# A transformer block in fp32: the last sequence's attention and shared experts moved in front of the routed experts

## The chip, the cores and the metric

The kernel runs on one core of a Trainium2 chip. The metric is the device time of one execution in microseconds. A core has TensorE (PE, matrix products; PEld is its weight load), VectorE (DVE), ScalarE (ACT), GpSimd (POOL) and SyncE (SP). The engines run their own instruction queues in order and wait for each other through semaphores. SP and ACT issue plain DMAs, POOL issues the indirect ones (gathers and scatters of rows).

## The reference

There are 16 sequences of 512 tokens with 256 channels, all fp32. The block normalizes, and adds to its input linear attention with 16 heads, a shared SwiGLU expert and routed experts (two groups of four, two experts of one group for each token):

```python
xn = layernorm(x)                                        # 16 x 512 x 256
q, k = elu(xn @ Wq + bq) + 1, elu(xn @ Wk + bk) + 1
v = xn @ Wv + bv
kv = einsum('bkhd,bkhm->bhdm', k, v)                     # by head, 16 x 16
att = einsum('bqhd,bhdm->bqhm', q, kv) / max(sum(q * sum_k k), 1e-6)
att = att @ Wo + bo
shared = swiglu(xn @ w_in.T) @ w_out.T                   # hidden 512
h = swiglu(xn @ w1.T)                                    # one hidden row for all routed experts
routed = sum over e of (h * w_se[:, e]) @ w2[e].T        # two weights per token are not zero
out = x + att + shared + routed
```

## The kernel before

**Sequences.** A loop over the 16 sequences (`for b in range(B)`, L992) computes for each one: the routed hidden rows `h` (`hidden_rows`, products `phr` on L587), written to the DRAM table `h_d`; the shared expert's hidden values `hs_all` (`hidden`, products `phs` on L613); and the attention. A row of `h_d` has 770 floats: 512 of `h`, 256 of the residual, and two routing weights. Both hidden layers go through `seven`, which forms two-by-two blocks with seven products for each half; its 14 products come in an order written out by hand, and after product number `n` it calls `then(n)`.

The attention needs only a small matrix for each sequence: `summarize` gives `xk` (L681), and `mix` makes of it `pvk` (L694, PE), `vk` (L703 and L708, DVE), `pm` (L713, PE) and `kvo` (L717, ACT). `outputs` then forms the sum of the shared expert and of the attention for a tile of 128 tokens in one PSUM group (L750): four products with `wout_sb` and two with `kvo`, each of which runs as two passes in fp32. `gather` adds that to the residual in `res` (L761) and stores it to `h_d` (L762).

**Routing.** `order` sorts the tokens by the pair of experts that they use, in pieces set between other work by `next(steps_of_order)`. There are 67 tiles of 128 slots that are always needed (`SURE`); a few more are run under `tc.If` if the counts ask for them (`rest`, L1061; its branch shows as L1063).

**Routed tiles.** A `Tiles` object holds two tiles. `rows()` gathers their rows from `h_d` by an indirect DMA on POOL for each tile (L902), into one of four buffers (the reused `qq_all`, `x_all`, `kk_all`, `xn_all`). `turn()` transposes the hidden half to `hT`: twelve copies on ACT (L923), four and three transposes on DVE (L929, L935); there are two `hT` buffers. `sums()` runs eight passes for each tile on PE with the weights of both experts (`py`, L952; `w2_sb` is shown as `w_sb`), then two DVE operations that bring in the gathered residual and weights (L959, L962), then scatters `y` to the output by an indirect DMA on POOL (L965). Rows are gathered three pairs ahead (`AHEAD = 3`), and turned two pairs ahead.

**The last sequence.** After its `hidden_rows`, the last four experts' weights are loaded over the space that held the weights of that layer (`load_expert`, L198, 16 DMAs on SP). Rows of the first three pairs are gathered before `hidden`. Its residual without attention and shared expert has been put into `h_d` early (L999). `mix` follows after four pairs of routed tiles (L1059), and the last sequence's outputs come at the very end: they are added to what the scatters left in the output, which is read back for that (`far`, L1081, `last`, L1088, stored on L1089).

**Order.** Each engine's order is made by a list scheduler of the language from the source order and the dependencies; `keep_in_program_order` fixes the order of the instructions given to it, `issue_after` puts one behind another, and `high_priority` draws instructions forward. PSUM has six banks for `ps_mm` and two for `ps_y`.

Of the kernel before, what the change touches and what calls it, by code (L numbers as in the profile page):

```python
# [10 lines left out]
FP = mybir.dt.float32  # L11
AF = mybir.ActivationFunctionType
ALU = mybir.AluOpType
AX = mybir.AxisListType

P = 128
# [5 lines left out]
def block_kernel(  # L22
# [29 lines left out]
    nc = tc.nc  # L52
    B, S, D = x.shape
# [3 lines left out]
    HID = w_out.shape[0]  # L57
    DH = 16
    KD = D // P
# [449 lines left out]
    def between(b, n):  # L509

        if b + 2 >= B:
            for _ in range(n or 0):
                next(steps_of_order)
# [84 lines left out]

        seven(f"phr_{b}", product, lambda a: a, room, done, lambda n: between(b, then(n)))

    def hidden(b, xs7):

        h = hs_all
        made = []

        def split(a):
            return a.rearrange("p (f j) -> p f j", f=2)

        def product(to, u, i, start, stop):


            for f in range(2):
                tc.keep_in_program_order(nc.tensor.matmul(  # L613
                    split(to)[:, f, :], lhsT=win_in[W7[i]][:, ts(2 * u + f, P)], rhs=xs7[i],
                    start=start and f == 0, stop=stop, skip_group_check=True,
                ))
# [30 lines left out]
    def first_hidden(xnT):  # L647

        more = weight_sums(win_in, win_12)
        for f in range(KH):  # L650
            both = []
            for w in ((win_in[0], win_in[1]), (win_12, win_in[2])):
                ph = ps_mm.tile([P, S], FP, tag="mm", name=f"phs_0_{f}_{len(both)}")
                for k in range(KD):
                    nc.tensor.matmul(
                        ph, lhsT=w[k][:, ts(f, P)], rhs=xnT[:, k, :], start=(k == 0), stop=(k == KD - 1)
                    )
                both.append(ph)
# [27 lines left out]
        nc.scalar.copy(xk, pxk)  # L686
        return xk

    def mix(b, xk, ksb):

        pvk = ps_mm.tile([P, KD, P], FP, tag="mm", name=f"pvk_{b}")
        for c in range(KD):
            for k in range(KD):
                nc.tensor.matmul(  # L694
                    pvk[:, c, :], lhsT=wv_sb[:, k, ts(c, P)],
                    rhs=by_quadrant(xk[:, k, :])[:, c],
                    start=(k == 0), stop=(k == KD - 1),
                )
        vk = one.tile([P, KD, P], FP, tag="vk", name=f"vk_{b}")

        with tc.high_priority():
            for c in range(KD):
                nc.vector.scalar_tensor_tensor(  # L703
                    vk[:, c, :].rearrange("p (q i) -> p q i", i=Q), by_quadrant(ksb)[:, c],
                    bv_sb[:, c : c + 1], pvk[:, c, :].rearrange("p (q i) -> p q i", i=Q),
                    ALU.mult, ALU.add,
                )
            nc.vector.tensor_tensor(  # L708
                vk, vk, headmask.unsqueeze(1).to_broadcast([P, KD, P]), ALU.mult
            )  # L710
        pm = ps_mm.tile([P, KD, D], FP, tag="mm", name=f"pm_{b}")
        for c in range(KD):
            nc.tensor.matmul(  # L713
                pm[:, c, :], lhsT=vk[:, c, :], rhs=wo_sb[:, c, :], start=True, stop=True
            )
# [23 lines left out]

    def outputs(b, t, qT, kvo, hs):  # L740


        if b + 2 < B or (b + 1 == B and t == 0):
            po = ps_y.tile([P, D], FP, tag="py", name=f"po_{b}_{t}")
        else:
            po = ps_mm.tile([P, D], FP, tag="mm", name=f"po_{b}_{t}")
        parts = [(hs[:, f, ts(t, P)], wout_sb[:, f, :]) for f in range(KH)]
        parts += [(qT[:, c, ts(t, P)], kvo[:, c, :]) for c in range(KD)]
        for i, (a, w) in enumerate(parts):
            step = nc.tensor.matmul(po, lhsT=a, rhs=w, start=(i == 0), stop=(i == len(parts) - 1))  # L750
            if b + 1 == B:
                tc.keep_in_program_order(step)
        return po

    def gather(b, res, qT, kvo, hs, placed, then):

        for t in range(NT):
            po = outputs(b, t, qT, kvo, hs)

            with tc.issue_after(placed.ins) if placed and t > 1 else nullcontext():  # L760
                nc.vector.tensor_tensor(res[:, t, 0:D], po, res[:, t, 0:D], ALU.add)  # L761
            nc.sync.dma_start(out=h_d[ts(b * NT + t, P), HID:ROW], in_=res[:, t, :])  # L762
            between(b, then(t))

    def order():

# [225 lines left out]
    for b in range(B):  # L992
        xn, xnT, _ = normed.pop(b)
        res, qq, kk = fronts.pop(b)
        if b + 1 < B:
            fronts[b + 1] = front(b + 1, normed[b + 1][1])
        if b + 2 == B:

            nc.sync.dma_start(  # L999
                out=h_d[ts(b + 1, S), HID:ROW].rearrange("(t p) h -> p t h", p=P), in_=fronts[b + 1][0]  # L1000
            )
            steps_of_order = order()
        if b + 1 == B:
            sums7 = token_sums(b, xnT)
            hidden_rows(b, sums7, {2: 2, 6: 2, 9: 2, 13: 2}.get)

            for e in waiting:
                load_expert(e)
            *lists, filled = next(steps_of_order)
            tiles = [Tiles(list(range(i, min(i + 2, SURE))), *lists) for i in range(0, SURE, 2)]  # L1010
        xk = summarize(b, xn, kk)
        if b == 0:
            sums = key_sum(0, kk)
            queries[0] = attend(0, qq, sums)
        if b + 2 < B:
            normed[b + 2] = normalize(b + 2)
        if b + 3 < B:
            xs[b + 3] = load_x(b + 3)
        if b == 0:
            first_rows(xnT)  # L1020
        elif b + 1 < B:
            sums7 = token_sums(b, xnT)
            hidden_rows(b, sums7, {9: 1}.get)
        ksb, (qT, turned) = sums, queries.pop(b)
        turned()
        if b + 1 < B:
            sums = key_sum(b + 1, fronts[b + 1][2])
# [18 lines left out]
        skip_runtime_bounds_check_because="whole tiles for all tokens, a part of a tile more for a pair",  # L1046
    )

    for i, w in enumerate(tiles[: AHEAD - 1]):

        w.turn(made[i])
    for g, w in enumerate(tiles):
        if g + AHEAD < len(tiles):
            tiles[g + AHEAD].rows()
        if g + AHEAD - 1 < len(tiles):
            tiles[g + AHEAD - 1].turn()
        w.sums()
        if g == AHEAD:
            kvo = mix(B - 1, xk, ksb)  # L1059

    def rest(i):  # L1061
        if i < TILES:
# [8 lines left out]
                    w.sums()  # L1071
                rest(i + STEP)


    first_po = outputs(B - 1, 0, qT, kvo, hs)
    rest(SURE)


    for half, queue in enumerate((nc.sync, nc.scalar)):
        far = work.tile([P, 2, D], FP, tag="hr", name=f"far_{half}", bufs=4)  # L1080
        queue.dma_start(  # L1081
            out=far, in_=out[B - 1, ts(half, 2 * P), :].rearrange("(t p) d -> p t d", p=P)
        )
        for j in range(2):
            t = 2 * half + j
            po = outputs(B - 1, t, qT, kvo, hs) if t else first_po
            y = work.tile([P, D], FP, tag="y", name=f"last_{t}", bufs=4)
            nc.vector.tensor_tensor(y, po, far[:, j], ALU.add)  # L1088
            (nc.sync, nc.scalar)[t % 2].dma_start(out=out[B - 1, ts(t, P), :], in_=y)  # L1089


# [30 lines left out]
```

## Time and profile before

| | |
|---|---|
| median of 3 runs | 1045.91 us (1045.9 to 1046.4) |
| the profiled execution's own time | 1045.97 us |
| its span, first to last instruction | 1044.2 us |
| mean granted TensorE clock | 0.992 |
| PE, DVE, ACT, POOL busy | 1011.8, 787.8, 479.1, 242.3 us |
| sequences, to the last `phs` product | 0 to 784.1 us |
| routed tiles | 792.5 to 1029.4 us |
| the last sequence's outputs and the end | 1029.4 to 1044.2 us |

The lines of a timeline read: start in us, duration, engine, source line, operation, output and inputs by name, shape, and how many instructions were merged; in brackets the idle time of the engine before it and what ended it. In a wait list the numbers are the total in us, how often, and the longest.

### The profile page before, as it was taken

To read this page: it belongs to the slowest core of one execution; us is meant where nothing else is said; L and a number is where in the kernel's file an instruction comes from. 1 tells how busy PE (TensorE), PEld (TensorE's weight loads), DVE (VectorE), ACT (ScalarE), POOL (GpSimd) and SP (SyncE) were. 2 spreads that over 40 slices of the span, in tenths; PEclk is the share of its full clock that TensorE was granted. 3 is DMA by queue.
4 is the path that set the end of the run, shared out by engine and by line. 5 is a ranking of instruction groups with operands and counts; after the bars stand their busy time and mean duration, and the time that the engine had idled before them with its cause. 6 is when DMAs were issued, how large, how long until landed. Compare 5 with 4: busy or idle time off the path is not lost. (4 is left out here: it accounts for less than half of the span.)

```text
span 1044.2 us, 12410 instructions
## 1 busy us (share of the span) xinstructions
PE 1011.8 (97%) x3704; PEld 685.2 (66%) x3704; DVE 787.8 (75%) x1976; ACT 479.1 (46%) x886; POOL 242.3 (23%) x353
## 2 busy tenths in 40 slices
PE   6999999999999999999999999999896999999998
PEld 4566868677786868686777768686672444444445
DVE  5969797978788797878786877868975666666662
ACT  2415353534344352535344443425138666667770
POOL 5202020110202021110202020211022555565541
PEclk9999999999999999999999999999998999999999
DMA  7142624425151523314141313221253445544441
GB/s 217 42 138 87 174 87 116 127 71 151 51 161 49 162 78 87 121 42 141 41 121 56 115 57 114 84 61 61 60 141 127 142 137 154 160 149 149 149 125 69
DMA packets 130436, 114.24 MB, mean 109 GB/s; under 512 B 72605, under 2 KB 114589, under 8 KB 130368
## 3 DMA queue, kind: packets, MB, share of 16 engines
q1 hardware_dynamic: 120080, 77.42, 25.3%
q0 software_dynamic: 8912, 35.21, 11.2%
q10 hardware_dynamic: 1376, 0.80, 0.3%
q8 instruction: 31, 0.51, 0.2%
q14 instruction: 37, 0.30, 0.1%
HBM read 63.52 MB, written 50.27 MB: 109 GB/s over the span
## 5 line engine op out<-in xcount | busy, mean ns | idle before, releaser
L952 PE MATMUL py<-w_sb,hT 128*128 x536 | 233.1, 598 | 8.4 <-DMA w_sb<-in_w 8.4
L952 PEld LDWEIGHTS py<-w_sb,hT 128*128 128x128 f32 x536 | 102.7, 192 | 137.7 <-issue 137.7
L750 PE MATMUL po<-wout_sb,hs_all 128*128 128x256 f32 x512 | 124.9, 382 | 1.9 <-DVE hs_all L572 1.4
L382 POOL TENSOR_TENSOR res<-x_all,bo_sb 128x256 f32<-128x256 f32 x64 | 49.0, 796 | 271.7 <-DMA h_d<-res 204.9
L750 PEld LDWEIGHTS po<-wout_sb,hs_all 128*128 128x128 f32 x512 | 95.8, 191 | 17.4 <-DVE hs_all L572 3.4
L965 POOL DMA_INDIRECT out<-y,goal x67 | 67.8, 1012 | 104.3 <-DVE y L962 95.1
L761 DVE TENSOR_TENSOR res<-po,res 128x256 f32<-128x256 f32 x60 | 25.5, 424 | 74.7 <-PE po L750 72.0
L668 POOL TENSOR_TENSOR k<-kk_all 128x512 f32<-128x512 f32 x16 | 20.9, 1309 | 261.8 <-DVE sm L450 251.9
L750 PE MATMUL po<-kvo,qT 128*128 128x256 f32 x256 | 65.9, 383 | 0.0
L587 PE MATMUL phr_w<-w_sb,ss 128*128 128x512 f32 x120 | 62.2, 600 | 3.6 <-DVE hr L566 2.2
L613 PE MATMUL phs_w<-ss,win_sb 128*128 128x256 f32 x240 | 61.6, 379 | 0.0
L613 PE MATMUL phs_t<-xnT,win_sb 128*128 128x256 f32 x240 | 61.6, 379 | 0.0
L587 PE MATMUL phr_t<-w_sb,xnT 128*128 128x512 f32 x120 | 61.3, 593 | 0.0
L404 PE MATMUL pk<-wkr_sb,xnT 128*128 128x266 f32 x240 | 58.9, 395 | 0.3 <-ACT xnT L305 0.3
L613 PE MATMUL phs_t<-ss,win_sb 128*128 128x256 f32 x240 | 59.1, 379 | 0.0
L587 PE MATMUL phr_t<-w_sb,ss 128*128 128x512 f32 x120 | 59.0, 593 | 0.0
L390 ACT ACTIVATE km<-km 128x1024 f32<-128x1024 f32 x16 | 16.9, 1058 | 90.7 <-DVE km L389 90.7
L681 PE MATMUL pxk<-kk_all,xn_all 128*128 128x256 f32 x256 | 57.9, 379 | 0.0
L923 ACT COPY hb<-qq_all 32x256 f32<-32x256 f32 x108 | 43.4, 402 | 26.2 <-DMA qq_all<-h_d,source 22.8
L415 PE MATMUL pq<-w_sb,xnT 128*128 128x256 f32 x240 | 54.2, 379 | 0.0
L750 PEld LDWEIGHTS po<-kvo,qT 128*128 128x128 f32 x256 | 47.5, 190 | 8.9 <-ACT kvo L717 3.0
L681 PEld LDWEIGHTS pxk<-kk_all,xn_all 128*128 128x128 f32 x256 | 48.6, 190 | 6.6
(215 smaller groups left out, 1936.3 us busy)
## 6 DMA issues: line engine op xcount, KB each, us to landing
h_d<-hr SPq DMA_DIRECT2D x64, 256.0 KB, 2.4
q_d<-qq_all SPq DMA_DIRECT2D x16, 512.0 KB, 2.8
qb<-q_d SPq DMA_DIRECT2D x64, 128.0 KB, 3.0
w_sb<-in_w SPq DMA_DIRECT2D x64, 128.0 KB, 3.5
h_d<-res SPq DMA_DIRECT2D x60, 129.0 KB, 1.9
x_all<-in_x SPq DMA_DIRECT2D x15, 512.0 KB, 5.3
xn_d<-xn_all SPq DMA_DIRECT2D x14, 512.0 KB, 3.5
xb<-xn_d SPq DMA_DIRECT2D x56, 128.0 KB, 3.0
```

Source lines behind the costliest of these rows:

```text
L382: nc.gpsimd.tensor_tensor(res[:, t, 0:D], xt[:, t, :], bo_sb, ALU.add)
L404: nc.tensor.matmul(pk, lhsT=xnT[:, k, ts(t, P)], rhs=wkr_sb[:, k, :], start=(k == 0), stop=(k == KD - 1),)
L415: nc.tensor.matmul(pq[:, t, :], lhsT=xnT[:, k, ts(t2 + t, P)], rhs=wq_sb[:, k, :], start=(k == 0), stop=(k == KD - 1),)
L587: tc.keep_in_program_order(nc.tensor.matmul(to, lhsT=xs7[i][:, ts(u, P)], rhs=w1_in[W7[i]], start=start, stop=stop, skip_group_check=True,))
L613: tc.keep_in_program_order(nc.tensor.matmul(split(to)[:, f, :], lhsT=win_in[W7[i]][:, ts(2 * u + f, P)], rhs=xs7[i], start=start and f == ...
L668: nc.gpsimd.tensor_tensor(k2, kk[:, 0:2, :], kk[:, 2:4, :], ALU.add)
L681: nc.tensor.matmul(pxk[:, c, :], lhsT=xn[:, t, ts(c, P)], rhs=kk[:, t, :], start=(t == 0), stop=(t == NT - 1),)
L750: step = nc.tensor.matmul(po, lhsT=a, rhs=w, start=(i == 0), stop=(i == len(parts) - 1))
L761: nc.vector.tensor_tensor(res[:, t, 0:D], po, res[:, t, 0:D], ALU.add)
L923: nc.scalar.copy(there[ts(q, Q), a - near, 0:n, :], self.hg[ts(a, Q), 0:n, ts(q, W)])
L952: nc.tensor.matmul(py.rearrange("p j d -> p (j d)"), lhsT=self.hT[:, f, ts(j, P)], rhs=w2_sb[:, f, bass.ds(regs[i % TR], 2 * D)], start=(f ...
L965: stored = nc.gpsimd.indirect_dma_start(out=out_rows, out_offset=bass.IndirectOffsetOnAxis(ap=self.goal[:, i : i + 1], axis=0), in_=y, in_ ...
```

## The change

The last sequence is treated like the others: its outputs are added to `res` and stored to `h_d` in front of the routed tiles, and the routed sums bring them to the output with the residual. `mix` is split into `values` and `mix`, which for the last sequence run after products 2 and 8 of `hidden`, with PSUM tiles from `ps_y`. A new `gather_last` does the outputs of all four tiles, first the products with `kvo`, then those with `wout_sb`, in two PSUM banks, with two adds and two stores. Since the rows of the first three pairs are gathered before these stores, they are gathered again afterwards, for their residual part: pairs 0 and 1 in front of the loop over the tiles, pair 2 in its first round, behind the gather of pair 3 and the turn of pair 2. The gather of pair 3 itself keeps its place in the source, which is now behind the stores. The part at the end that reads the output back is gone.

```diff
-    def hidden(b, xs7):
+    def hidden(b, xs7, then=lambda n: None):
...
-        seven(f"phs_{b}", product, split, room, done, lambda n: None)
+        seven(f"phs_{b}", product, split, room, done, then)
         return h, made
...
-    def mix(b, xk, ksb):
-        pvk = ps_mm.tile([P, KD, P], FP, tag="mm", name=f"pvk_{b}")
+    def small_sums(b, shape, name):
+        if b + 1 == B:
+            return ps_y.tile(shape, FP, tag="py", name=f"{name}_{b}"), tc.keep_in_program_order
+        return ps_mm.tile(shape, FP, tag="mm", name=f"{name}_{b}"), lambda step: step
+
+    def values(b, xk, ksb):
+        pvk, pin = small_sums(b, [P, KD, P], "pvk")
...
+        return vk
+
+    def mix(b, vk):
+        pm, pin = small_sums(b, [P, KD, D], "pm")
...
-        nc.scalar.copy(kvo, pm)
+        with tc.high_priority() if b + 1 == B else nullcontext():
+            nc.scalar.copy(kvo, pm)
         return kvo
...
+    def gather_last(b, res, qT, kvo, hs):
+        pos = [ps_y.tile([P, 2, D], FP, tag="py", name=f"po_{b}_{i}") for i in range(NT // 2)]
+        def add(parts, t, begin, end):
+            for i, (a, w) in enumerate(parts):
+                tc.keep_in_program_order(nc.tensor.matmul(
+                    pos[t // 2][:, t % 2, :], lhsT=a, rhs=w, start=begin and i == 0 and t % 2 == 0,
+                    stop=end and i == len(parts) - 1, skip_group_check=True,
+                ))
+        for t in range(NT):
+            add([(qT[:, c, ts(t, P)], kvo[:, c, :]) for c in range(KD)], t, True, False)
+        for t in range(NT):
+            add([(hs[:, f, ts(t, P)], wout_sb[:, f, :]) for f in range(KH)], t, False, True)
+        for i, po in enumerate(pos):
+            to = res[:, 2 * i : 2 * i + 2, 0:D]
+            with tc.high_priority():
+                nc.vector.tensor_tensor(to, po, to, ALU.add)
+            nc.sync.dma_start(
+                out=h_d[ts(b * NT // 2 + i, 2 * P), HID:ROW].rearrange("(t p) h -> p t h", p=P),
+                in_=res[:, 2 * i : 2 * i + 2, :],
+            )
...
-        hs, made = hidden(b, sums7) if b else first_hidden(xnT)
         if b + 1 < B:
-            kvo = mix(b, xk, ksb)
+            hs, made = hidden(b, sums7) if b else first_hidden(xnT)
+            kvo = mix(b, values(b, xk, ksb))
+        else:
+            def then(n):
+                if n == 2:
+                    made_of["vk"] = values(b, xk, ksb)
+                if n == 8:
+                    made_of["kvo"] = mix(b, made_of["vk"])
+            made_of = {}
+            hs, made = hidden(b, sums7, then)
+            kvo = made_of["kvo"]
...
-        if b + 1 < B:
+        if b + 1 == B:
+            for i, w in enumerate(tiles[: AHEAD - 1]):
+                w.turn(made[i])
+            gather_last(b, res, qT, kvo, hs)
+        else:
             gather(b, res, qT, kvo, hs, normed[b + 2][2]() if b + 2 < B else None, {0: 2, 1: 2, 3: 2}.get)
...
-    for i, w in enumerate(tiles[: AHEAD - 1]):
-        w.turn(made[i])
+    for w in tiles[: AHEAD - 1]:
+        w.rows()
     for g, w in enumerate(tiles):
         if g + AHEAD < len(tiles):
             tiles[g + AHEAD].rows()
         if g + AHEAD - 1 < len(tiles):
             tiles[g + AHEAD - 1].turn()
+        if g == 0:
+            tiles[AHEAD - 1].rows()
         w.sums()
-        if g == AHEAD:
-            kvo = mix(B - 1, xk, ksb)
...
-    first_po = outputs(B - 1, 0, qT, kvo, hs)
     rest(SURE)
-    for half, queue in enumerate((nc.sync, nc.scalar)):
-        far = work.tile([P, 2, D], FP, tag="hr", name=f"far_{half}", bufs=4)
...
-            po = outputs(B - 1, t, qT, kvo, hs) if t else first_po
-            y = work.tile([P, D], FP, tag="y", name=f"last_{t}", bufs=4)
-            nc.vector.tensor_tensor(y, po, far[:, j], ALU.add)
-            (nc.sync, nc.scalar)[t % 2].dma_start(out=out[B - 1, ts(t, P), :], in_=y)
```

More of the change, by code (lines that the diff above doesn't have):

```diff
@@ L687, in summarize @@
         return xk
-    def mix(b, xk, ksb):
-        pvk = ps_mm.tile([P, KD, P], FP, tag="mm", name=f"pvk_{b}")
+    def small_sums(b, shape, name):
[4 more added lines that the diff above has]
+        pvk, pin = small_sums(b, [P, KD, P], "pvk")
         for c in range(KD):
             for k in range(KD):
-                nc.tensor.matmul(
+                pin(nc.tensor.matmul(
                     pvk[:, c, :], lhsT=wv_sb[:, k, ts(c, P)],
@@ L697, in mix @@
                     start=(k == 0), stop=(k == KD - 1),
-                )
+                ))
         vk = one.tile([P, KD, P], FP, tag="vk", name=f"vk_{b}")
@@ L710, in mix @@
             )
-        pm = ps_mm.tile([P, KD, D], FP, tag="mm", name=f"pm_{b}")
+        return vk
+    def mix(b, vk):
+        pm, pin = small_sums(b, [P, KD, D], "pm")
         for c in range(KD):
-            nc.tensor.matmul(
+            pin(nc.tensor.matmul(
                 pm[:, c, :], lhsT=vk[:, c, :], rhs=wo_sb[:, c, :], start=True, stop=True
-            )
+            ))
         kvo = one.tile([P, KD, D], FP, tag="kvo", name=f"kvo_{b}")
-        nc.scalar.copy(kvo, pm)
+        with tc.high_priority() if b + 1 == B else nullcontext():
+            nc.scalar.copy(kvo, pm)
         return kvo
@@ L740, in outputs @@
     def outputs(b, t, qT, kvo, hs):
-        if b + 2 < B or (b + 1 == B and t == 0):
+        if b + 2 != B:
             po = ps_y.tile([P, D], FP, tag="py", name=f"po_{b}_{t}")
@@ L749, in outputs @@
         for i, (a, w) in enumerate(parts):
-            step = nc.tensor.matmul(po, lhsT=a, rhs=w, start=(i == 0), stop=(i == len(parts) - 1))
-            if b + 1 == B:
-                tc.keep_in_program_order(step)
+            nc.tensor.matmul(po, lhsT=a, rhs=w, start=(i == 0), stop=(i == len(parts) - 1))
         return po
@@ L763, in gather @@
             between(b, then(t))
+    def gather_last(b, res, qT, kvo, hs):
[5 more added lines that the diff above has]
+                    stop=end and i == len(parts) - 1, skip_group_check=True,
+                ))
+        for t in range(NT):
[10 more added lines that the diff above has]
+            )
     def order():
@@ L1072, in rest @@
                 rest(i + STEP)
-    first_po = outputs(B - 1, 0, qT, kvo, hs)
     rest(SURE)
-    for half, queue in enumerate((nc.sync, nc.scalar)):
-        far = work.tile([P, 2, D], FP, tag="hr", name=f"far_{half}", bufs=4)
[L1081 to L1085, printed above, removed]
-            po = outputs(B - 1, t, qT, kvo, hs) if t else first_po
-            y = work.tile([P, D], FP, tag="y", name=f"last_{t}", bufs=4)
-            nc.vector.tensor_tensor(y, po, far[:, j], ALU.add)
-            (nc.sync, nc.scalar)[t % 2].dma_start(out=out[B - 1, ts(t, P), :], in_=y)
 def kernel(**inputs):
```

## The prediction

> **What bounds the kernel now.** I read four views, from wide to narrow: the busy shares of the page, PE's waits in the stretch where the last sequence gives way to the routed experts, the table of windows there, and the timelines of PE and of the tail.
>
> ```profile
> PE 1011.8 (97%) x3704; PEld 685.2 (66%) x3704; DVE 787.8 (75%) x1976; ACT 479.1 (46%) x886; POOL 242.3 (23%) x353
> ```
> PE is busy for 97% of the span: time falls only where PE idles, runs at a low clock, or where the span goes on after it. Between 745 and 860 us the waits say where it idles:
>
> ```profile
> PE py L952 <- DMA w_sb<-in_w: 8.4, 1, 8.4
> ...
> PE pm L713 <- DVE vk L708: 2.2, 1, 2.2
> ```
> The first routed product waits 8.4 us for the last expert weights; `mix` of the last sequence, placed among the routed tiles, waits 2.2 us for DVE. PE's timeline gives the places:
>
> ```profile
> 783.08 1.03 PE L613 MATMUL phs_t<-xnT,win_sb 128*128 128x256 f32 x4
> 792.48 30.38 PE L952 MATMUL py<-w_sb,hT 128*128 x64 [8.37 <-DMA w_sb<-in_w]
> 822.69 1.05 PE L694 MATMUL pvk<-xk,wv_sb 128*128 128x128 f32 x8
> 825.91 1.10 PE L713 MATMUL pm<-wo_sb,vk 128*128 128x256 f32 x4 [2.17 <-DVE vk L708]
> ```
> The table of windows (busy us by engine, then granted clock, DMA share, GB/s) shows what the gap does to the clock:
>
> ```profile
> 784.00:792.40 8.40, 0.10 (x1) 0.00 (x0) 6.83 (x16) 7.96 (x19) 0.25 (x1) 0.72 0.84 285
> 792.40:799.00 6.60, 6.53 (x9) 2.80 (x10) 1.36 (x4) 6.36 (x17) 0.00 (x0) 0.59 0.01 2
> ```
> and the same table for the stretches after and within two shorter gaps:
>
> ```profile
> 736.80:739.00 2.20, 2.15 (x5) 1.82 (x6) 2.20 (x5) 0.07 (x1) 0.00 (x0) 0.50 0.00 0
> ...
> 823.60:825.90 2.30, 0.14 (x2) 0.02 (x1) 2.21 (x7) 0.47 (x2) 1.09 (x2) 1.00 0.66 212
> ```
> After the gap PE has a clock of 0.59 over 6.6 us, 2.9 us lost. The stretch from 736.8 follows a gap of 2.47 us and also has half clock; the last row is the gap of 2.17 us, which lost none. Last, the tail:
>
> ```profile
> 1029.41 1.89 PE L750 MATMUL po<-wout_sb,hs_all 128*128 128x256 f32 x8
> ...
> 1030.89 0.98 POOL L965 DMA_INDIRECT out<-y,goal  x1 [2.46 <-DVE y L962]
> ...
> 1032.62 1.97 PE L750 MATMUL po<-wout_sb,hs_all 128*128 128x256 f32 x8 [0.45 <-PEq L1063]
> ...
> 1035.25 0.43 ACTq L1081 DMA_DIRECT2D far<-out  x1
> ...
> 1038.25 1.09 DVE L1088 TENSOR_TENSOR last<-po,far 128x256 f32<-128x256 f32 x3 [7.63 <-DMA far<-out]
> ...
> 1040.66 0.42 DVE L1088 TENSOR_TENSOR last<-po,far 128x256 f32<-128x256 f32 x1 [1.33 <-PE po L750]
> ```
> The routed products end at 1029.41, the last scatter is issued at 1030.89, and then come 10.3 us of products for the last sequence, an add and a store. The span ends at 1044.2: 14.8 us after the last routed product.
>
> **The change, part by part.** PE's amount of work stays; it is moved. I lay out PE's new order on the old times.
>
> *Mix goes into `hidden`.* Its 8 and 4 products took 0.90 us (822.69 to the idle) and 0.94 us; `hidden` then ends at 784.1 + 1.8 = 785.9. The 2.17 us bubble goes, if `vk` is ready between product 2 (about 775) and product 8 (about 780.5). DVE idles for 5.64 us before 778.72, and `vk` takes 1.0 us (0.60 + 0.43). Without that cover it costs the old 2.2 us. `kvo`'s copy (0.59 us) fits between ACT's copies, which have gaps of 1 to 2 us there.
>
> *The 48 output passes go in front.* At the tail a run of 12 takes 2.59 us (1035.28 to 1037.87), so four take 10.35 us: 785.9 to P = 796.2. The query half stands first and lasts 3.45 us; it covers the rest of `hs_all`, whose last product is written 3.3 us after `hidden` ends now (787.4 against 784.1), so I count no wait. If that were uncovered, it would be some 3 us. The expert weights are in by 792.4, and ACT and DVE have the first pair's `hT` ready at 790.9, later by at most the 1.8 us that `hidden` is longer. Neither holds up P. So PE fills the 8.37 us gap, and stays warm.
>
> *Routed products.* From 826.85 to 1029.41 there are 59 tiles, 3.433 us each; 67 take 230.0 us: P + 230.0 = 1026.2. Against 1029.41 that is 3.2 us earlier: 8.37 (gap) + 2.9 (clock) + 2.17 (bubble) - 10.35 (moved in), 3.1.
>
> *The second gathers.* They need the two new stores. After P: an add of 128x512 on DVE (0.68, as L571), an SP issue and landing (129 KB took 1.9 us, 256 KB 2.4), a POOL wake: gathers start at about P + 3.6. On SP the stores stand behind 16 expert issues, the last at 780.9, so nothing delays them, and nothing follows them. On POOL eight gathers now stand in a row: pairs 0 and 1 again, pair 3 (issued at 782 to 783 before, hidden then), pair 2 again. At 0.97 us plus 0.3 between them that is 1.27 each. Base values of tile 0 come at P + 7.6, where `y` could have used them at P + 3.4. Behind that wait on DVE stand only transposes for pair 2, which PE needs at P + 13.7 and which take 2.9 us; six `ps_mm` banks let PE run to P + 20.6 without any `y`. So the wait for base values is hidden.
>
> What is late next is `hT` of pairs 3 and 4. Pair 3: second gather issued at P + 3.6 + 5 x 1.27 = P + 10.0, landing after 4.0 (ACT started at 811.67 on a gather issued at 807.68), ACT copies 5.0, a last DVE transpose 0.6: P + 19.6; PE wants it at P + 20.6. Pair 4: its two gathers alternate with two scatters behind the eight, so the second starts 11 slots after the first: P + 17.6; landing P + 21.6, ready P + 27.2; wanted at P + 27.5. From pair 5 on POOL needs 5.2 us a pair and PE 6.87, so slack grows. Slack of 1.0 and 0.3 us is nothing to rely on. No row shows eight gathers in a row on idle DMA: the eight beside the expert loads landed in up to 8.7 us, single ones in 3.9. Bounds: 0 (landing 4.0) to 4.4 + 2.9 us (landing 8.4 and a cold restart). 394 KB (128 rows of 770 floats) each 1.27 us is 310 GB/s, and the DMA moved 348 to 362 GB/s just before 790, so I sit near the single gather: 0.5 us.
>
> Two rules of the Trainium skill bear on this. "DMA: Bandwidth & Descriptors", the anatomy of a DMA on the GpSimd path, gives about 2.0 us fixed plus bytes at 436 GB/s: 2.9 us for a gather, so pair 4 would have 1.4 us of slack and the stall would be 0. The row says 3.9 to 4.0; I keep the row. "TensorE: Matmul & The Clock Gate", Part 1, says the clock halves after an idle window of some 3.4 us and returns after 3.4 us of work. By it the gap cost 1.7 us and a stall under 3.4 us costs nothing extra. Here the gap cost 2.9, and 2.47 us of idling was already enough for half clock (1.5 us lost by 741). So the gain in clock is larger than the rule makes it, and so is the price of a medium stall.
>
> *The tail.* The last `y` and scatter keep their distance: issue 1.48 us after the last product, landing 3.1 to 3.4 later, so 4.9. Before, the last store was issued at 1041.1, landed after 1.7, and the span ended 1.4 later. After: 1026.2 + 0.5 + 4.9 + 1.4 = 1033.0. The conditional tiles remain and are skipped; PE's own wait there was 0.45 us, beside the scatter. Bounds of the end: 1.4 less (nothing after landing) to 2 more (the branch outlasting the scatter: the far load went out at 1035.2, 0.9 after landing).
>
> **Sum**: span 1044.2 - 1033.0 = 11.2 us less. The profiled execution took 1045.97, so 1034.8; it stands 0.06 over the median of 1045.91, which changes nothing.
>
> **The rivals.** *A: a stall at pair 3 or 4.* For it: slack below 1 us, and 8.7 us landings earlier. Against: then the expert loads shared the DMA. With landings of 6.5 us the stall is 2.2 to 3 us plus 1.5 to 2.9 of clock: 1034.8 + 4.5 = 1039.3.
>
> *B: the gap is not filled.* It would be that output products wait for `kvo` or `hs_all`, or that the order of instructions comes out otherwise than the source suggests, so that PE idles some 3 us and goes cold, 2.9: 1040.7. The long idle of DVE speaks against.
>
> *C, the other side: the re-gather chain becomes the bound.* The stores now depend on PE's output, and gathers, ACT and DVE follow serially: 19.6 us for pair 3 against PE's cover of 20.6. It decides when pair 3 or 4 is late by 11.7 - 2.9 = 8.8 us, so gathers would have to land after 12.5 us, or scatters that wait for base values would have to stand ahead of pair 3 on POOL (2.6 us and their wait of 4) and landings double as well. At 11 us late it gives 1034.3 + 11 + 2.9 = 1048.2. Nothing lands that late in the trace.
>
> *D: the tail drains more slowly,* by up to 2 us, if the skipped branch outlasts the scatter: 1036.8. The far load's 0.9 us speaks for it.
>
> **How the numbers follow.** My forecast, with D inside it, has 0.68: 1032.5 to 1037. A 0.15, B 0.10, C 0.07. The range 1032.5 to 1040 holds the first and most of A and B, 0.88, less what either side may miss. Within 0.2% (about what a measurement of this kernel can tell) needs a loss of 9 to 13 us by chance: 0.02, out of B. Faster 0.91, slower 0.07.
>
> **What would show it.** Right: no PE wait for `w_sb`; output products directly after `phs` with a clock near 1.00 until 800; no `pm` wait; first `py` near 796; last scatter within 7 us of the end; six more gathers on POOL. Wrong: PE waiting for `hT` between 815 and 830 (A, C), idle before or between the output products (B), or over 7 us from the last product to the end (D).

## The result, and the profile after

| | before | after |
|---|---|---|
| median, measured side by side | 1046.16 us (1045.9 to 1048.25, 4 runs) | 1039.12 us (1038.63 to 1040.87, 4 runs) |
| ratio after to before | | 0.9931, 95% interval [0.9914, 0.9949] |
| the profiled execution's own time | 1045.97 us | 1038.63 us |
| its span | 1044.2 us | 1036.9 us |

The change makes the kernel 7.0 us faster; 11.2 were forecast. The profiled execution took 3.8 us more than the 1034.8 predicted, which lies inside the range of 1032.5 to 1040. The views below, in the order of those before, show where. First the page's busy shares:

```profile
PE 1006.9 (97%) x3704; PEld 682.8 (66%) x3704; DVE 789.1 (76%) x1974; ACT 479.0 (46%) x886; POOL 248.0 (24%) x359
```
PE issues as many products as before and is busy 4.9 us less; the 2.9 us lost at half clock are part of that. POOL has six instructions more, the second gathers. Now the stretch between the last sequence and the routed tiles, in PE's waits from 745 to 860 us (total, how often, longest):

```profile
PE py L985 <- DVE hT L968: 1.6, 2, 1.0
```
The waits for `w_sb` and for `vk` are gone. A new one has come, for `hT`. PE's timeline shows where:

```profile
779.79 1.03 PE L723 MATMUL pm<-wo_sb,vk 128*128 128x256 f32 x4
...
784.10 1.03 PE L613 MATMUL phs_t<-xnT,win_sb 128*128 128x256 f32 x4
784.97 3.62 PE L780 MATMUL po<-kvo,qT 128*128 128x256 f32 x16
788.42 7.07 PE L780 MATMUL po<-wout_sb,hs_all 128*128 128x256 f32 x32
795.33 20.76 PE L985 MATMUL py<-w_sb,hT 128*128 x48
817.12 7.11 PE L985 MATMUL py<-w_sb,hT 128*128 x16 [1.03 <-DVE hT L968]
824.80 35.43 PE L985 MATMUL py<-w_sb,hT 128*128 x82 [0.57 <-DVE hT L968]
```
`pm` runs among the `phs` products with no wait; the 48 output passes stand exactly in the old gap; the routed products follow at 795.33 without a pause. Eight passes make a tile, so the first wait is after six tiles, at pair 3, and the second after two more, at pair 4. The table of windows (busy us by engine, granted clock, DMA share, GB/s) gives the clock:

```profile
784.00:796.00 12.00, 12.00 (x56) 10.34 (x55) 9.20 (x20) 11.41 (x27) 0.00 (x0) 1.00 0.36 119
796.00:805.00 9.00, 9.00 (x22) 3.99 (x21) 1.50 (x3) 4.89 (x13) 3.51 (x4) 1.00 0.42 122
...
815.00:825.00 10.00, 8.40 (x20) 3.38 (x19) 5.91 (x14) 7.03 (x18) 6.53 (x7) 1.00 0.69 202
```
PE is full and at full clock where it had idled and then run at 0.59. The two short waits cost no clock.

Why `hT` of pair 3 is late can be read on three engines, SP, POOL and ACT:

```profile
795.48 2.05 SPq L793 DMA_DIRECT2D h_d<-res  x2
```
```profile
800.57 0.94 POOL L935 DMA_INDIRECT qq_all<-h_d,source  x1 [19.57 <-DMA h_d<-res]
...
806.85 0.95 POOL L935 DMA_INDIRECT xn_all<-h_d,source  x1 [0.30 <-issue]
808.11 1.04 POOL L998 DMA_INDIRECT out<-y,goal  x1 [0.30 <-DVE hT L968]
...
814.58 0.97 POOL L935 DMA_INDIRECT qq_all<-h_d,source  x1 [0.30 <-issue]
```
```profile
811.52 4.98 ACT L956 COPY hb<-xn_all 32x256 f32<-32x256 f32 x12 [10.45 <-DMA xn_all<-h_d,source]
```
POOL had waited 19.57 us for the stores and starts at 800.57. Six gathers follow each other (pairs 0, 1 and 3, two tiles each). The sixth, pair 3's second, goes out at 806.85; ACT starts on it 4.67 us later. Then come a scatter, three more gathers and another scatter, and the second gather of pair 4 (into `qq_all` again) goes out only at 814.58. Last the tail: POOL's last scatter, then what POOL's sequencer does on the line of the branch (L1112), then at the program's end (L1152). These rows give the minimum, median and maximum duration in ns and the first and last start in us:

```profile
1028.92 0.98 POOL L998 DMA_INDIRECT out<-y,goal  x1 [2.45 <-DVE y L995]
```
```profile
L1112 POOLq EVENT_SEMAPHORE  x4: 17/42/43, 1031.2 to 1031.5; - x4
...
L1112 POOLq INC_SWDGE_SEM  x1: 1007/1007/1007, 1031.6 to 1031.6; - x1
```
```profile
L1152 POOLq DRAIN  x3: 51/103/3418, 1032.6 to 1036.6; - x3
```
At the branch POOL waits until the last scatter has landed (1031.2, which is 2.3 us after its issue), spends 1.0 us on a queue's semaphore (`INC_SWDGE_SEM`), and then has a `DRAIN`, an instruction of the program's end, of 3.4 us until 1036.0. The span ends at 1036.9, 8.0 us after the issue of the last scatter.

### The profile page after: what moved, and what is told of

The parts are those of the page before. It is cut to its first block, busy times and chain, and to the rows that moved or that the text cites. A ratio compares the mean times of both kernels' runs of the same rounds, so it can differ in the third digit from the quotient of the medians.

```text
span 1036.9 us, 12401 instructions
## 1 busy us (share of the span) xinstructions
PE 1006.9 (97%) x3704; PEld 682.8 (66%) x3704; DVE 789.1 (76%) x1974; ACT 479.0 (46%) x886; POOL 248.0 (24%) x359
## 5 line engine op out<-in xcount | busy, mean ns | idle before, releaser
L985 PE MATMUL py<-w_sb,hT 128*128 x536 | 230.7, 592 | 1.6 <-DVE hT L968 1.6
L760 PE MATMUL po<-wout_sb,hs_all 128*128 128x256 f32 x480 | 116.6, 380 | 1.4 <-DVE hs_all L572 1.4
L760 PEld LDWEIGHTS po<-wout_sb,hs_all 128*128 128x128 f32 x480 | 89.2, 190 | 15.1 <-DVE hs_all L572 3.4
L760 PE MATMUL po<-kvo,qT 128*128 128x256 f32 x240 | 61.8, 383 | 0.0
L404 PEld LDWEIGHTS pk<-wkr_sb,xnT 128*128 128x128 f32 x240 | 46.5, 194 | 9.0 <-ACT xnT L305 0.5
```

Source lines behind the costliest of these rows:

```text
L404: nc.tensor.matmul(pk, lhsT=xnT[:, k, ts(t, P)], rhs=wkr_sb[:, k, :], start=(k == 0), stop=(k == KD - 1),)
L985: nc.tensor.matmul(py.rearrange("p j d -> p (j d)"), lhsT=self.hT[:, f, ts(j, P)], rhs=w2_sb[:, f, bass.ds(regs[i % TR], 2 * D)], start=(f ...
```

## The experiments

Three questions were open: what the second gathers cost, what the branch costs in the tail, and what the two parts of the early gain, filling the gap and keeping the clock, are worth. The ratios are to the kernel before, run beside each kernel on the same chip.

A warning first. The first four kernels here (`e1_no_if`, `e2_pair3_early`, `e3_mix_alone`, `e4_warm`) ran on one chip and the last one (`e12_first_pair`) on another, and no run of the changed kernel is on record for either. In the traces of these five, DVE stands still between 781 and 834 us for up to 7.3 us (1.6 in `e4_warm`), although what it needs should be there by the times of the products; and they hold 7,349 to 7,601 records of DMA completions, where the other nine traces hold 8,352 to 8,448 and show no such stop. The kernel before ran on both of these chips too, and was not slower there (medians 1046.11 and 1046.50 us, 1045.83 and 1046.27 on two others), but its traces from there were not kept. So these five are read by what their own traces show, not by their distance from the changed kernel.

**1. No conditional tiles** (`e1_no_if`). The changed kernel without them:

```diff
-    rest(SURE)
+    del rest
```


> The changed kernel without the conditional tiles behind tile 66 (they are skipped with these inputs, so nothing that runs is left out but the branch). In the changed kernel the span ends 9.45 us after the last routed product, where the prediction had 6.3. Theory 1, the branch: engines step over the skipped block after the last scatter, and the end waits for it. Then the distance falls to about 6.3 us and the time by 3 us. Theory 2, the end itself: something behind the last indirect DMA on POOL costs these 3 us in every program; before, it lay beside the last sequence's outputs. Then the distance stays above 8.5 us and the time within 1 us of the changed kernel's.

Measured: 1042.99 us (1042.7 to 1044.04), ratio 0.997 [0.996, 0.9981]. Its tail, POOL's last scatter and the rows of the program's last line:

```profile
1035.87 0.98 POOL L998 DMA_INDIRECT out<-y,goal  x1 [2.45 <-DVE y L995]
```
```profile
L1152 POOLq DRAIN  x3: 46/109/4642, 1035.6 to 1040.8; - x3
```
The drain begins at 1035.6, beside the last scatter, and lasts 4.64 us: it ends 4.4 us after the issue, and the span 5.2 us after it (1041.1), against 8.0 with the branch. So the branch costs 2.75 us in the tail: it holds POOL until the scatter has landed and puts its own 1.0 us and the drain behind that. The whole kernel was nevertheless slower than the changed one elsewhere, because PE waits 4.91 us at pair 4 and is cold afterwards (half clock for 3.4 us):

```profile
818.04 7.10 PE L985 MATMUL py<-w_sb,hT 128*128 x16 [0.94 <-issue]
830.05 30.26 PE L985 MATMUL py<-w_sb,hT 128*128 x66 [4.91 <-DVE hT L968]
```
```profile
826.99 1.78 DVE L962 STREAM_TRANSPOSE hT<-qq_all 32x256 f32<-32x256 f32 x4 [7.30 <-remote]
```
DVE stood still for 7.3 us before these transposes (`remote`: a semaphore was raised just before, by no instruction that the profile can name), while ACT had begun to copy the same gathered rows at 820.14.

**2. Pair 3 gathered early and again** (`e2_pair3_early`), which keeps pair 3's `hT` out of the row of gathers behind the stores:

```diff
-            for w in tiles[:AHEAD]:
+            for w in tiles[: AHEAD + 1]:
...
-        if g + AHEAD < len(tiles):
+        if g and g + AHEAD < len(tiles):
...
-        if g == 0:
-            tiles[AHEAD - 1].rows()
+        if g < 2:
+            tiles[g + AHEAD - 1].rows()
```


> The changed kernel, with the rows of pair 3 gathered in front of the stores, as in the kernel before, and a second time behind its turn. Theory 1, the chain: store, gather in POOL's queue, ACT copies and DVE transposes of pairs 3 and 4 are what PE waits for (1.03 and 0.57 us at 817 and 824). Pair 3 leaves that chain and pair 4's gathers move forward by one or two places of 1.27 us: both waits go, and the time falls by 1.6 us. Theory 2, DMA load: the waits come from the number of gathers in flight, which rises by two here; then a wait of 1 us or more stays in front of pair 3 or 4, or moves to pair 5.

Measured: 1044.71 us (1041.69 to 1048.12), ratio 0.9986 [0.9976, 0.9996]. A miss: pair 3's wait is gone, but PE waits 1.56 us at pair 2 and 1.94 at pair 4, with half clock after it, and DVE again stands still (6.6 us before 825.96, 4.1 before 833.86). Nothing about the gathers follows from this run.

**3. `mix` alone** (`e3_mix_alone`): the kernel before, with only `mix` moved into `hidden`, by the same edit as in the change.

> One part alone: the kernel before, with the products of mix of the last sequence inside hidden, and all else as before (the outputs stay at the end). Theory: the wait of 2.17 us at 825.9 goes, and mix's 1.8 us of products move into the gap in front of the routed tiles, which shrinks from 8.4 to about 6.5 us as the weights' arrival does not move. Time 4.0 us less than before. Rival: the products inside hidden wait for vk or delay hs_all, and the gap does not shrink: 2 us less or nothing.

Measured: 1043.74 us (1042.69 to 1046.59), ratio 0.9979 [0.9971, 0.9986], 2.4 us less where 4.0 were expected. The 2.17 us wait of `pm` is gone. The gap did not get shorter, though; it ends on another wait:

```profile
795.28 65.00 PE L963 MATMUL py<-w_sb,hT 128*128 x146 [9.36 <-DVE hT L946]
```
```profile
786.23 0.69 DVE L571 TENSOR_TENSOR hs_all<-hs_all,phs_w 128x512 f32<-128x512 f32 x1 [4.15 <-PE phs_t L613]
```
The same add had waited 0.42 us in the kernel before and waits 1.3 in the changed one. DVE stood still here as in the two kernels above, and pair 0's `hT` came behind it. So the run shows that the bubble goes. Its time is no measure of it: the first routed product starts 2.8 us later than in the kernel before (795.28 against 792.48), against 4.2 us of `mix` and bubble taken out behind it (822.69 to 826.85). The rest of the expectation could not be seen.

**4. A warm gap** (`e4_warm`): the kernel before, with 18 products without use in the gap.

```diff
+            warm = ps_y.tile([P, D], FP, tag="py", name="warm")
+            for i in range(WARM):
+                tc.keep_in_program_order(nc.tensor.matmul(
+                    warm, lhsT=ident, rhs=wout_sb[:, i % KH, :], start=(i == 0), stop=(i == WARM - 1)
+                ))
```


> The kernel before, with 18 products (36 passes, 7.8 us) on constants in the gap of 8.4 us in front of the routed tiles; their result is not used. Nothing else is moved. Theory: the clock alone. PE stays warm, the first routed products run at full clock, and the time falls by the 2.9 us that the low clock cost, with the first routed product still at 792.5. By the 3.4 us of warm-up that the skill's page gives, the gain would be 1.7 us. Rival: it makes the first routed product later, or the clock drops anyway: no gain.

Measured: 1044.71 us (1042.93 to 1047.65), ratio 0.9985 [0.9976, 0.9994].

```profile
793.37 27.70 PE L953 MATMUL py<-w_sb,hT 128*128 x64 [1.46 <-DMA w_sb<-in_w]
```
The same 64 passes had taken 30.38 us: the clock is worth 2.7 us. The time fell by 1.4 only; 0.9 of the difference is that the first product starts 0.9 later (793.37 against 792.48; the wait is still for the weights), the other 0.4 is not explained.

**5. The changed kernel again** (`after_again`), beside the next three.

> The changed kernel itself once more, on the chip of the three that follow, for their comparison and for the spread of its waits: the runs e1_no_if and e2_pair3_early were each slower than the one profile of the changed kernel had led me to expect, by waits of ACT and DVE on no semaphore near 820 to 827 us. If the changed kernel has these now and then too, its time should spread up to 1043; if the waits belong to the place of the instructions in those two kernels, it stays at 1038.5 to 1041 with waits of 1.0 and 0.6 us in front of pairs 3 and 4.

Measured: 1040.46 us (1039.29 to 1042.34), ratio 0.9939 [0.9922, 0.9956]; waits for `hT` of 1.8 us in all, and 8.0 us from the last scatter to the end. It is the measure for kernels 6 to 8.

**6. No conditional tiles, and DVE's instructions shifted** (`e6_shift`): kernel 1 with 48 tiny memsets on DVE among the `phs` products, to see whether its stop belongs to a place in DVE's instruction stream.

```diff
+                if n == 3:
+                    for _ in range(FILL):
+                        tc.keep_in_program_order(nc.vector.memset(filler, 0.0))
...
-    rest(SURE)
+    del rest
```


> e1_no_if with 48 small DVE memsets of one column spread over 775 to 796 us, so that all later DVE instructions stand 48 places further on in DVE's instruction stream; nothing else differs. In e1_no_if DVE stood still from 820.1 to 827.0 us with its semaphores reached, while two instruction fetches (queue 14) came in at 822, and PE then waited 4.9 us. Theory 1, instruction delivery: the halt belongs to a place in the stream, so it goes or moves away from pair 4 for DVE (ACT may keep its own), and the time falls from 1043.0 by 3 to 6 us. Theory 2, load of the gathers: the halt belongs to the time and the transfers there, and stays at pair 4.

Measured: 1037.99 us (1036.72 to 1039.78), ratio 0.9915 [0.9898, 0.9932]. No stop; waits of 1.31 and 0.81 us as in the changed kernel; 5.2 us from the last scatter to the end. By the medians it is 2.5 us under the changed kernel on this chip, which fits the 2.75 us of the branch; with four executions each the intervals overlap, so the tail's own rows are the better evidence. That no stop appears fits the expectation, but no kernel on this chip has one, so the shift is not shown to be the reason.

**7. The branch early** (`e7_if_early`): the conditional tiles in front of the products of the last tile, which loads its register again; the conditional tiles get buffers of their own (both not printed here).

```diff
+        if g + 1 == len(tiles):
+            rest(SURE)
         w.sums()
...
-    rest(SURE)
```


> The changed kernel with the conditional tiles in front of the last tile instead of behind it (they still are skipped with these inputs); the last tile loads its register again, and the conditional pairs use buffers of their own. In the changed kernel POOL waits at the branch for the last scatter to land, and only then runs its closing semaphore and a drain of 3.4 us. Theory 1: without the branch behind it the drain runs beside the last scatter, as in e1_no_if, where the span ended 6.7 us after the last product instead of 9.45. The branch then costs PE about 0.5 us in front of the last tile, and the time falls by 2 us. Theory 2: the drain's time belongs to the end of any program with a conditional block, and the distance stays above 9 us.

Measured: 1039.7 us (1038.36 to 1040.2), ratio 0.9932 [0.9916, 0.9949]. The tail is 5.3 us after the last scatter, but PE now waits at the branch:

```profile
PE py L988 <- DVEq L1104: 1.6, 1, 1.6
```
DVE reaches the branch only at 1027.5, behind the `y` of the tile before, and PE waits for it there. Of 2.7 us, 1.6 went into this new wait where 0.5 had been expected. The medians differ by 0.8 us, which lies within the intervals.

**8. Gathered once** (`e8_gather_once`): the second gathers left out, so that the first six tiles lack attention and shared expert of the last sequence's tokens.

```diff
-    for w in tiles[: AHEAD - 1]:
-        w.rows()
...
-        if g == 0:
-            tiles[AHEAD - 1].rows()
```


> The changed kernel without the second gathers: the first six tiles take the residual of their first gather, in which the last sequence's rows lack attention and shared expert. Six gathers of 1.27 us less stand on POOL, and the gathers of pair 3 are the first behind the stores. Theory 1, POOL's queue: pair 3 lands 5 us earlier, pair 4 too, no wait in front of them is left, and the time falls by the 1.6 us of these waits. Theory 2, the waits come from stores or transfers and not from the queue: a wait of 1 us stays in front of pair 3.

Measured: 1037.73 us (1037.01 to 1039.45), ratio 0.9919 [0.9901, 0.9937], 2.7 us under the changed kernel on this chip by the medians (the intervals overlap). PE has no wait at all from 780 us to the end:

```profile
796.62 53.81 PE L985 MATMUL py<-w_sb,hT 128*128 x125
```
So the waits at pairs 3 and 4 come from the second gathers. Whether by their places in POOL's queue or by the load of their transfers, this run cannot tell, since both are gone; the next kernels keep all gathers and change the order.

**9, 10 and 11. Another order on POOL**, beside the changed kernel a third time (`e11_after_third`). `e9_order` gathers pair 3 first behind the stores, and pair 2 again one round later; `e10_both` has the early branch as well.

```diff
-    for w in tiles[: AHEAD - 1]:
+    for w in (tiles[AHEAD], *tiles[: AHEAD - 1]):
         w.rows()
...
-        if g + AHEAD < len(tiles):
+        if g and g + AHEAD < len(tiles):
...
-        if g == 0:
+        if g == 1:
             tiles[AHEAD - 1].rows()
```


> Here only the order of POOL's queue behind the stores changes: pair 3's gathers go in front of the second gathers of pairs 0 and 1, and the second gathers of pair 2 go behind the first gather of pair 4. Theory 1 (pairs 3 and 4 are late because their gathers stand in POOL's row of some 1.27 us each): pair 3's gathers go out 5 us earlier and its wait of 0.9 to 1.0 us is gone; pair 4's second gather moves up one place only, 1.3 us, so its wait of 0.6 to 1.0 us shrinks to 0 to 0.6. In all 1 to 1.6 us less than the changed kernel, which gives a ratio near 0.9925 to the kernel before. Base values of tile 0 come 2.6 us later, which the six ps_mm banks still cover. Theory 2 (what decides these waits is a halt of DVE or ACT that moves with the instruction stream): the waits stay at 1.5 us in all or come elsewhere, 1 to 5 us, with `issue` or `remote` named as what ended an engine's idle time; the time is the changed kernel's or up to 4 us more.

> The order of POOL of the kernel with pair 3 first, and the conditional tiles in front of the last tile's products. Theory 1 (two separate costs, that add up): the tail falls from 9.5 to 6.8 us behind the last product, PE waits 1.6 us at the branch as it did with the early branch alone, so 0.8 to 1.1 us less than with the order alone, and about 2.2 us less than the changed kernel: near 1037.5, a ratio of 0.9915. Theory 2 (halts of DVE or ACT move with the instruction stream): the branch's place shifts nothing in front of it, so the routed part is the same as with the order alone, whatever that is, and only the tail differs, by 0.8 to 1.1 us.

> The changed kernel once more, on the chip of the two kernels before it, to have a difference without a change of chip. Both theories: 1039 to 1041, a ratio of 0.993 to 0.994 to the kernel before, waits for hT of 0.9 to 1.0 us at pair 3 and 0.6 to 1.0 at pair 4, and 9.5 us behind the last product.

Measured: the changed kernel 1038.93 us (1038.29 to 1039.23), ratio 0.9934 [0.992, 0.9947]; `e9_order` 1039.8 (1038.79 to 1040.72), 0.9945 [0.9931, 0.9958]; `e10_both` 1039.22 (1038.26 to 1040.53), 0.994 [0.9926, 0.9953]. A miss, and an instructive one. PE's and DVE's timelines of `e9_order`:

```profile
811.98 58.60 PE L985 MATMUL py<-w_sb,hT 128*128 x136 [2.29 <-DVE hT L968]
```
```profile
808.01 0.48 DVE L992 SCALAR_TENSOR_TENSOR y<-py,qq_all 128x256 f32<-128x256 f32 x1 [10.44 <-DMA qq_all<-h_d,source]
808.53 0.48 DVE L995 SCALAR_TENSOR_TENSOR y<-py,qq_all,y 128x256 f32<-128x256 f32 x1
808.93 1.77 DVE L962 STREAM_TRANSPOSE hT<-kk_all 32x256 f32<-32x256 f32 x4
810.73 1.10 DVE L968 STREAM_TRANSPOSE hT<-hb 128x256 f32<-128x256 f32 x3
```
No wait is left at pairs 3 and 4. But tile 0's base values come at 808.01 instead of 804.51, and on DVE the transposes of pair 2 stand behind them, until 811.8; PE wants them at 809.7. That wait also hides what the new order did: pair 3's `hT` is ready at 816.4, just when PE would have come without it, but pair 4's only at 824.4, when PE would have come at 823.3. So the order helped pair 3; pair 4 does not wait because PE is 2.3 us late. One wait of 2.3 us stands in place of two of 1.4 together: 0.9 us more, as much as the medians differ, though within the intervals. The expectation had asked only whether `ps_mm` covers a late `y`, and not what stands behind `y` on its engine. `e10_both` is 0.6 us under `e9_order` by the medians, again within the intervals.

**12. Pair 0 first, then pair 3, then pair 1** (`e12_first_pair`), with the early branch.

```diff
-    for w in (tiles[AHEAD], *tiles[: AHEAD - 1]):
+    for w in (tiles[0], tiles[AHEAD], *tiles[1 : AHEAD - 1]):
         w.rows()
```


> Like the kernel with pair 3's gathers in front and the early conditional tiles, but pair 0's second gathers come first on POOL, then those of pair 3, then pair 1. Theory 1 (the 2.2 us wait at pair 2 in that kernel came because pair 2's transposes stand on DVE behind tile 0's base values, which its order brought 2.5 us later; POOL's order decides all these waits): tile 0's base values come at about 804.6 to 805 again, pair 2 does not wait; pair 3's second gather goes out at about 804.5 instead of 807.0, which is 2.5 us more room than in the changed kernel, so its wait of 0.9 is gone; pair 4's second gather goes out at 813.5 instead of 814.6, and its wait is 0 to 0.4. With 1.6 us at the branch and a tail of 6.8 us, the time is about 2 us less than the changed kernel's, a ratio of 0.991 to 0.992. Theory 2 (a wait of 1 to 2 us comes out somewhere whatever the order, because gathers, ACT and DVE together have no room): PE waits 1 to 2.3 us for hT in front of 830 again, and the ratio is 0.993 to 0.994.

Measured: 1046.25 us (1044.81 to 1047.45), ratio 0.9998 [0.9989, 1.0007]: not faster than the kernel before. Its timelines of PE and DVE:

```profile
796.09 27.63 PE L988 MATMUL py<-w_sb,hT 128*128 x64
829.79 40.50 PE L988 MATMUL py<-w_sb,hT 128*128 x88 [6.08 <-DVE hT L971]
```
```profile
820.99 0.48 DVE L995 SCALAR_TENSOR_TENSOR y<-py,kk_all 128x256 f32<-128x256 f32 x1 [5.22 <-PE py L988]
...
826.74 1.78 DVE L965 STREAM_TRANSPOSE hT<-qq_all 32x256 f32<-32x256 f32 x4 [4.75 <-remote]
```
The first eight tiles run through with no wait: with all six gathers kept, pair 3's `hT` is ready at 814.9, where PE wants it at 816.7. So it is the place in POOL's queue that had made pair 3 late. Then DVE stands still twice, before 820.99 for products of tile 4 that PE had finished at about 813, and before 826.74. It looks like the stop of kernels 1 to 4. Whether this order beats the changed kernel on a chip without the stop was not tried and stays open.

## Why the prediction was right, point by point

The range of 1032.5 to 1040 held, and the gains came as reckoned. The forecast inside it (1034.8, up to 1037 with rival D) did not: the 1038.63 of the profiled execution is rivals A and D together. The prediction's own signs of being wrong say the same: PE waited for `hT` between 815 and 830 us, and the last scatter was 8.0 us from the end instead of within 7.

**The output passes in the gap: right.** The routed products were to begin at P = 796.2; they begin at 795.33. The whole last sequence stands 0.7 us earlier in this execution (`hidden` begins at 771.08 against 771.81), which is luck (see the clock), so P is right to 0.2 us. The output passes took 10.36 us where 10.35 were reckoned. The query half did cover `hs_all`, and `kvo` did not hold it up. Rival B is out.

**The clock: right.** 2.9 us were counted, 1.00 was granted throughout the stretch, and `e4_warm` puts 2.7 on it by itself. "TensorE: Matmul & The Clock Gate", Part 1 of the Trainium skill, would have given 1.7 us, an estimate from its half clock for some 3.4 us; the row was the better guide. What the prediction made of the short gap is too strong, though: "2.47 us of idling was already enough for half clock". All 14 traces have this gap of 2.47 or 2.48 us near 737 us. In six of them PE has half clock right behind it, in eight it does not. The changed kernel's profile is one of the eight:

```profile
736.80:739.00 2.20, 2.20 (x11) 1.94 (x11) 2.20 (x4) 0.59 (x1) 0.00 (x0) 1.00 0.00 0
```
The kernel before has 0.50 in this row. So whether a gap of this length costs clock changes from execution to execution. The head start comes from it: it is 0.2 us before this gap, 1.7 behind it, and later waits take 1.0 back.

**The bubble of `pm`: right.** No wait in the profile after, and none in `e3_mix_alone`.

**The wait for base values on DVE: right, but nearly used up.** It is 7.39 us in front of 804.51, with nothing late on PE. The values came at P + 9.2 instead of P + 7.6, and pair 2's transposes behind them ended at 808.33, 0.7 us before PE wanted them. `e9_order` shows how near it was: 3.5 us later it costs 2.3 us.

**The slack of pairs 3 and 4: too small a cost, rival A in part.** The step put the gathers at P + 3.6; they start at P + 5.2. The add of the second bank, costed as if DVE were free, starts 1.1 us after P, behind a transpose that waits for ACT:

```profile
796.10 0.45 DVE L968 STREAM_TRANSPOSE hT<-hb 128x256 f32<-128x256 f32 x1 [0.64 <-ACT hb L956]
796.46 0.65 DVE L792 TENSOR_TENSOR res<-po,res 128x512 f32<-128x512 f32 x1
```
From the end of that add to POOL's start are 3.5 us instead of the 2.9 reckoned. The spacing of 1.27 us was right to 0.02. From pair 3's second gather to ACT's start passed 4.67 us, not 4.0. So pair 3 was 2.2 us later than reckoned at ACT (1.5 at the issue, 0.7 in the landing), and its slack of 1.0 became a wait of 1.0. From 795.33 to 824.80 PE takes 29.5 us for eight tiles, which need 27.5: the stall costs 2.0 us, not 0.5. `e8_gather_once` shows the cause by taking it away, and `e12_first_pair` by the order alone for pair 3. The clock stayed at 1.00 after both waits, which was not certain: in `e7_if_early` it is 0.50 from 755 to 757 us, behind a gap of 1.91 us.

**The tail: rival D, and more of it.** The scatter was to land 3.4 us after its issue and the end to come 1.4 later, 4.8 together; it is 8.0. The two microseconds set aside for the branch were the right mechanism and too small: the branch costs 2.75 us (8.0 against 5.2 in `e1_no_if` and `e6_shift`). The step looked for the branch as a delay beside the scatter. What costs the time is the order on POOL: landing, then the branch, then a drain that otherwise runs beside the scatter. The scatter itself landed 2.3 us after its issue, sooner than the 3.4 reckoned. In the kernel before, the branch was passed while PE still had outputs to compute, so only PE's own wait of 0.45 us there was on the path.

**The sum.** 1033.0 was predicted for the end of the span: -0.9 for P, +1.5 for the stall, +3.2 for the tail give 1036.8; it is 1036.9. Without the head start it would have been some 0.7 us more. Rival C did not happen: pair 3 was late by 1 us, not by 8.8.

## What to carry to other kernels

When work moves off the tail, what was hidden beside it becomes the tail: here a branch that waits for the last scatter and a drain behind it took back 2.75 us. When a store and gathers are put ahead of a pipeline, follow each engine's queue, not only the data: an add behind one transpose, six gathers at 1.26 us and transposes behind a waiting `y` decided the waits. Slack under one microsecond, worked out from single transfers, should be booked as a cost.

## What the runs showed of the hardware that was not expected

- At the end of the program POOL's drain takes 3.4 us behind the conditional in the changed kernel and 2.9 us in the kernel before; it takes 4.6 us in `e1_no_if`, `e6_shift` and `e7_if_early`, where it begins beside the last scatter. The passed-over conditional costs POOL 1.0 us more once the last scatter has landed.
- Half clock lasted 3.4 us after the 4.9 us wait in `e1_no_if`. Waits of 1.0 and 0.6 us cost no clock in the changed kernel's profile. The same gap of 2.47 us was followed by half clock in six traces and not in eight.
- In the five kernels named above DVE stood still in the stretch where the indirect gathers begin. Up to 775 us their traces hold about as many DMA completions as the others; from there to the end about two fifths are missing (1,519 in `e1_no_if` where the changed kernel has 2,474). In `e12_first_pair` PE's semaphore increments for tiles 5, 6 and 7 are recorded together, at 826.71, 826.81 and 826.90, while the last products of these tiles began at 816.26, 819.69 and 823.12; DVE starts again at 826.74. In `e1_no_if` the three stand at 826.97, 827.07 and 827.16, and DVE starts again at 826.99. In the changed kernel each is recorded 0.6 us after its last product began. That points to signals from PE arriving late, not to DVE's own instructions, but it is read from two traces with missing records. The kernel before is the only one that ran on both kinds of chip, and it was equally fast on both; without its traces from there, whether the chip, the kernel or both together decide stays open.
